# Deformable attention on one core: the stored dot products get two copies of their first and last line, and are read back in fewer pieces

## The chip, the cores and the metric

The kernel runs on one core of a Trainium2 chip. A core has TensorE (PE in the profile, its weight loads PEld), VectorE (DVE), ScalarE (ACT), GpSimd (POOL) and SyncE (SP), each with an instruction queue of its own that it works off in order. Here SP, ACT and POOL issue DMAs; sixteen DMA engines carry them out. The metric is the time on the device of one execution, in microseconds (us), as the median of several runs. Less is better.

## What is computed

The reference is two layers on x of shape (2, 64, 64, 256): a deformable attention, a graph-routed mixture of four experts, a shifted-window attention, and a mixture of eight experts. The change concerns the first of these. Cut to what matters, with eight groups g of 32 channels and nine sampling points k:

```
qkv = dwconv3x3(layernorm(x) @ qkv_w + qkv_b)
off[g]  = offsets from q, plus the 3x3 grid times (2g+1)
mask    = nine factors a pixel, from q
k_s     = bilinear(k_map[g], y + off_y, x + off_x) * mask     # 9 samples a pixel
v_s     = bilinear(v_map[g], y + off_y, x + off_x) * mask     # coordinates clipped to the image
attn    = softmax(q . k_s / sqrt(32))
out[g]  = sum over k of attn * v_s
x       = x + out @ proj_w + proj_b
```

Coordinates are clipped to the image: a sample above the first line takes the first line, one below the last takes the last.

## The kernel before, in words

The kernel samples without a gather. The offsets move a sample by less than one pixel from its grid place (the kernel has another path for the other case), so a sample is a weighted sum of 3x3 neighbours of that place. With r = 2g+1, a group needs key and value lines at y + (ky-1)r + sy-1 with ky and sy from 0 to 2: nine lines a row.

`static_attention` (line 470 on) runs n from -2 to 7 over the groups in the order 1, 2, ..., 7, 0. In each n it mixes three lanes of steps: the values of one group (`group_values`), the weights of the next (`group_weights`) and the dot products of the one after (`group_dots`). Each lane has a place in the order between 0 and 1 for each step (lines 515 to 525: values 0.12 + 0.88f, weights 0.04 + 0.8f, dots 0.95f), the steps are sorted by it and recorded. A scheduler that estimates durations then sets the final order on each engine and gives the DMAs of SP and ACT their completion semaphores.

`group_dots` (L538): `keys` and `queries` load key columns (L565) and query columns (L556) by SP. `multiply` (L570) forms, for two x at a time, the dot products of each of 64 rows (times 2 images: 128 partitions) with all 64 key lines and three neighbouring x on PE (L578), and copies them from PSUM to the tile `stage` on ACT (L585; in the first two n every second copy is DVE's). Eight such steps fill a tile of 64 lines x 3 x 32; two of these tiles are in use in turn. `store` (L590) writes them to the DRAM tile `dots` of the group from ACT's queue (L594): four DMAs of 16 rows, each with only those lines that its rows can need. A group has six such stores, group 0 four.

`group_weights` (L614): `read(ky)` (L672) picks, for each row y, its own three lines from `dots` into the tile `lk` (two in use), with all six column blocks. The address moves by one row and one line from one partition to the next, so rows of the same distance are one DMA of SP (`pick`, L655; L669). Where a line would lie outside the image the pick takes the first or last line; there the three lines are picked one by one, and the rows are cut where clipping begins and into multiples of 16 and a rest. `read_near` (L681) does it for group 0, five lines one by one. DVE multiplies the picked lines with bilinear weights and adds them up (L707, L711, L716, L720, L721), a softmax follows (L725 to L736), and DVE and POOL form the weights of the value lines (L746 to L776), which POOL writes to the DRAM tile `wd` (L786).

`group_values` (L854): SP loads values (L871), DVE spreads them (L876), POOL loads the weights of 16 rows in dense form (L882) into one of two `mat` tiles, and PE multiplies (L907) and accumulates over 18 columns and three kx. `clear` (L887) begins an accumulation with matmuls of a zero stationary operand `none` and, as moving operand, the first 512 columns of the constants `cstt`. ACT copies the sums out and stores them (L916, L919).

`cstt` holds constants of later stages; it is loaded at L206 at the very start and lies in SBUF to the end. `metaformer` (L2558) calls the stages: position table, first attention, projection and router, first experts, second attention, last experts.

Of the kernel before, what the change touches and what calls it, by code (L numbers as in the profile page):

```python
# [23 lines left out]
F32 = mybir.dt.float32  # L24
# [43 lines left out]
WB = W + 2 * BORDER  # L68
XH, XQ = W // 2, W // 4
ORDER = list(range(1, G)) + [0]  # L70
BAND = 16
# [122 lines left out]
class Net:  # L194
    def __init__(self, ctx, tc, I, out):
        self.tc, self.nc, self.I, self.out = tc, tc.nc, I, out
        self.const = ctx.enter_context(tc.tile_pool(name="const", bufs=1))
        nc = self.nc
        self.ident = self.const.tile([P, P], F32, name="ident")
        make_identity(nc, self.ident)  # L200
        self.colt = self.const.tile([P, NCOLS], F32, name="colt")
        nc.sync.dma_start(self.colt, I["cols"])
        self.rowt = self.const.tile([P, NROWS], F32, name="rowt")
        nc.scalar.dma_start(self.rowt, I["rows"].to_broadcast([P, NROWS]))
        self.cstt = self.const.tile([P, NCST], F32, name="cstt")
        nc.sync.dma_start(self.cstt, I["cst"])  # L206

# [330 lines left out]
    def group_dots(self, g, qd, kd, own, dots, pools, alone):  # L538
# [8 lines left out]
        runs = [(-2, 0), (1, 1)] if near else [((kx - 1) * r - 1, kx) for kx in range(3)]  # L547
        dots[g] = s = pools["dram"].tile([H, B, 6, H, 3, XH], F32, name="dots")
        two, steps, box = pools["first"], [], {}
# [20 lines left out]
        def multiply(h, dx, i0):  # L570
            kt, qt = box[h, dx], box["q", h]
            if i0 == 0:
                box["d"] = two.tile([P, H, 3, XH], F32, name="stage")
            ps = [pools["dot"].tile([P, 2, 3 * H], F32, name="dot") for _ in range(2)]
# [7 lines left out]
            for jj in range(2):  # L582
                x = XQ * jj + i0

                (nc.vector.tensor_copy if alone and jj else nc.scalar.copy)(  # L585
                    box["d"][:, :, :, x : x + 2],
                    ps[jj].rearrange("p i (s y) -> p y s i", s=3),
                )

        def store(h, at):  # L590
            for y in range(0, H, BAND):

                lo, hi = max(0, y - r - 1), min(H, y + BAND + r + 1)
                ins = nc.scalar.dma_start(  # L594
# [10 lines left out]
        for n, (h, dx, at) in enumerate(todo):  # L605
            if n == 1:
                steps.append(lambda: queries(1))
            if n + 2 < len(todo):
                steps.append(lambda n=n: keys(*todo[n + 2][:2]))
            steps += [lambda h=h, dx=dx, i=i: multiply(h, dx, i) for i in range(0, XQ, 2)]  # L610
            steps.append(lambda h=h, at=at: store(h, at))
        return steps

    def group_weights(self, g, offd, mask, low, edge, s, wd, none, pools):  # L614
# [39 lines left out]

        def pick(to, dy, first, blocks, n, y0=0, y1=H):  # L655

            for b in range(B):
                y = y0
                while y < y1:
                    ky = min(max(y + dy, 0), H - 1)  # L660
                    inside = 0 < y + dy < H - 1
                    end = min(y1, H - 1 - dy) if inside else (min(y1, 1 - dy) if y + dy <= 0 else y1)
                    if end - y > 16:
                        end -= (end - y) % 16
                    src = bass.AP(
                        s.tensor, s.offset + y * stride + b * (stride // B) + first * block + ky * line,
                        [[stride + (line if inside else 0), end - y], [block, blocks], [1, n * XH]],
                    )
                    nc.sync.dma_start(to[H * b + y : H * b + end], src)  # L669
                    y = end  # L670

        def read(ky):  # L672
            box[ky] = lk = two.tile([P, 6, 3, 3, XH], F32, name="lk")
            dy = (ky - 1) * r
            y0, y1 = max(0, 1 - dy), min(H, H - 1 - dy)
            pick(lk.rearrange("p k y s x -> p k (y s x)"), dy - 1, 0, 6, 9, y0, y1)
            for sy in range(3):
                for lo, hi in ((0, y0), (y1, H)):
                    pick(lk[:, :, sy].rearrange("p k s x -> p k (s x)"), dy + sy - 1, 0, 6, 3, lo, hi)

        def read_near():  # L681
# [172 lines left out]
    def group_values(self, g, vd, wd, mats, none, odd, sums, od, pools):  # L854
# [1703 lines left out]
def metaformer(ctx: ExitStack, tc: tile.TileContext, I, out):  # L2558
# [110 lines left out]
```

## Time and profile before

| | us |
|---|---|
| median of 3 runs | 5531.37 (5528.46 to 5539.13) |
| the profiled execution | 5531.03 |
| its span from first to last instruction | 5529.2 |

| stage, us from the start | length | PE | DVE | ACT | POOL | clock | DMA share | GB/s |
|---|---|---|---|---|---|---|---|---|
| 0 to 1090: edge sort, maps of q, k, v, offsets | 1090 | 937 | 822 | 178 | 96 | 0.88 | 0.61 | 131 |
| 1090 to 2470: first attention | 1380 | 960 | 400 | 314 | 478 | 0.81 | 0.74 | 187 |
| 2470 to 2660: projection, router | 190 | 96 | 74 | 19 | 37 | 0.74 | 0.52 | 143 |
| 2660 to 3500: graph edges | 840 | 404 | 339 | 24 | 399 | 0.72 | 0.16 | 30 |
| 3500 to 3780: first experts alone | 280 | 258 | 59 | 67 | 4 | 0.96 | 0.70 | 215 |
| 3780 to 5040: second attention beside experts | 1260 | 1136 | 635 | 568 | 247 | 0.94 | 0.44 | 135 |
| 5040 to 5529: last experts | 489 | 368 | 151 | 94 | 134 | 0.89 | 0.79 | 254 |

The columns of engines are busy us in the stage, clock is the share of full TensorE clock that was granted, and DMA share is the mean busy share of the sixteen DMA engines. An idle time of an engine is put down to what ended it: "PE dot L578 <- ACT stage L585: 209.5, 29, 27.9" reads as 209.5 us in 29 waits, the longest 27.9 us. A name with q (SPq, ACTq) is an engine's queue while it waits or issues a DMA, which does not count as busy.

### The profile page before, as it was taken

What the parts mean: (1) busy time and instruction counts of PE and PEld (TensorE: products, weight loads), DVE (VectorE), ACT (ScalarE), POOL (GpSimd) and SP (SyncE); (2) the same over time, 40 slices, a digit from 0 to 9 for tenths busy, and PEclk for the clock granted to TensorE, in tenths of its full rate; (3) what the DMA queues carried; (4) which work ended last, traced back from release to release, by engine and by line L of the source; (5) the groups of instructions that cost most, each with busy time, mean ns of one, the idle gap of its engine ahead of it and who ended that gap; (6) DMA issues with size and microseconds to landing.
All of it is one profiled execution on the core that took longest, in us unless ns stands there. A gap on an engine that the chain in (4) does not pass through costs nothing. (4 is left out here: it accounts for less than half of the span.)

```text
span 5529.2 us, 64325 instructions
## 1 busy us (share of the span) xinstructions
PE 4158.5 (75%) x22555; PEld 2930.8 (53%) x22555; DVE 2481.4 (45%) x5535; ACT 1264.3 (23%) x2432; POOL 1395.6 (25%) x1769
## 2 busy tenths in 40 slices
PE   7899999468677776554436670698999879998695
PEld 4565579355455554334213340586666546667584
DVE  5788888454322322203424481123444465543233
ACT  2221111022232222000200000123445344443121
POOL 3100000103344433422365406202120232101224
PEclk8898999668888888777768895899999889999898
DMA  8533368957888887665200003675454335445996
GB/s 227 169 118 105 104 138 82 118 152 182 208 210 216 210 225 178 151 144 164 13 5 5 4 1 108 207 232 185 130 148 120 94 119 155 131 127 155 306 308 202
DMA packets 752557, 808.72 MB, mean 146 GB/s; under 512 B 360516, under 2 KB 629280, under 8 KB 736466
## 3 DMA queue, kind: packets, MB, share of 16 engines
q1 hardware_dynamic: 590942, 477.93, 32.9%
q0 software_dynamic: 67552, 199.30, 14.5%
q10 hardware_dynamic: 93716, 127.14, 7.6%
q8 instruction: 184, 3.01, 0.2%
q14 instruction: 163, 1.34, 0.1%
HBM read 495.83 MB, written 312.33 MB: 146 GB/s over the span
## 5 line engine op out<-in xcount | busy, mean ns | idle before, releaser
L578 PE MATMUL dot<-kt,qt 64*128 64x192 f32 x2944 | 415.3, 398 | 322.0 <-ACT stage L585 209.5
L907 PE MATMUL acc<-mat,vt 128*64 128x192 f32 (+2 forms) x3680 | 531.8, 440 | 99.8 <-DMA mat<-wd 58.0
L578 PEld LDWEIGHTS dot<-kt,qt 64*128 64x128 f32 x2944 | 348.6, 227 | 418.6 <-ACT stage L585 243.8
L1415 PE MATMUL ps<-oh,ol 128*128 128x512 f32 (+1 forms) x864 | 358.0, 578 | 244.8 <-DVE oh L1408 166.8
L907 PEld LDWEIGHTS acc<-mat,vt 128*64 128x64 f32 x3680 | 300.6, 155 | 292.2 <-issue 185.7
L585 ACT COPY stage<-dot 128x384 f32<-128x384 f32 x640 | 275.7, 500 | 781.0 <-PE dot L578 446.9
L1415 PEld LDWEIGHTS ps<-oh,ol 128*128 128x128 f32 x864 | 179.0, 210 | 423.5 <-issue 307.0
L1689 PE MATMUL ps_h<-xgT,w1t 128*128 128x256 f32 x1216 | 320.1, 388 | 36.0 <-ACT hT L1692 25.4
L1825 PE MATMUL ps_y<-w2t,hT 128*128 128x256 f32 x1216 | 309.7, 406 | 41.7 <-ACT hT L1817 41.7
L1813 PE MATMUL ps_h<-xgT,w1t 128*128 128x256 f32 x1216 | 311.4, 399 | 34.9 <-ACT hT L1817 14.1
L1697 PE MATMUL ps_y<-w2t,hT 128*128 128x256 f32 x1216 | 305.8, 385 | 10.0 <-issue 8.8
L2432 POOL DMA_INDIRECT xs<-tn,sloti x128 | 124.3, 971 | 747.1 <-DVE slot L2430 676.4
L273 DVE SCALAR_TENSOR_TENSOR cv<-pad,colt,cv 128x2048 f32<-128x2048 f32 x128 | 298.8, 2348 | 0.0
L1825 PEld LDWEIGHTS ps_y<-w2t,hT 128*128 128x128 f32 x1216 | 239.0, 202 | 92.2 <-ACT hT L1817 48.4
L1813 PEld LDWEIGHTS ps_h<-xgT,w1t 128*128 128x128 f32 x1216 | 227.3, 196 | 99.8 <-ACT hT L1817 29.7
L1854 POOL DMA_INDIRECT back<-ys,back_row x128 | 134.3, 1049 | 560.6 <-DVE ex L1612 277.9
L437 PE MATMUL ps_k<-padk,diag 128*128 128x512 f32 x576 | 268.9, 626 | 0.2 <-ACT km L442 0.2
L1692 ACT ACTIVATE hT<-ps_h,b1t 128x256 f32<-128x256 f32 x304 | 143.9, 476 | 540.8 <-PE ps_h L1689 349.6
L1689 PEld LDWEIGHTS ps_h<-xgT,w1t 128*128 128x128 f32 x1216 | 230.0, 195 | 69.0 <-ACT hT L1692 27.5
L1697 PEld LDWEIGHTS ps_y<-w2t,hT 128*128 128x128 f32 x1216 | 234.5, 193 | 44.7 <-issue 10.3
L1299 PEld LDWEIGHTS <-ol 128*128 128x128 bf16 x1792 | 225.2, 148 | 38.7 <-issue 28.3
L1299 PE MATMUL psc<-oh,ol 128*128 128x64 bf16 x1792 | 236.4, 305 | 8.5 <-DVE oh L1297 8.5
(413 smaller groups left out, 6797.3 us busy)
## 6 DMA issues: line engine op xcount, KB each, us to landing
w1t<-in_W SPq DMA_DIRECT2D x152, 512.0 KB
w2t<-in_W SPq DMA_DIRECT2D x152, 512.0 KB
xg<-xs SPq DMA_DIRECT2D x152, 256.0 KB
kt<-kd SPq DMA_DIRECT2D x92, 288.0 KB
pr<-stage SPq DMA_DIRECT2D x16, 1584.0 KB
mat<-wd POOLq DMA_DIRECT2D x56, 384.0 KB
b2t<-in_b SPq DMA_DIRECT2D x152, 128.0 KB
ys<-y ACTq DMA_DIRECT2D x76, 256.0 KB
```

The lines of the kernel that those rows point to most:

```text
L273: nc.vector.scalar_tensor_tensor(out, src, w, out, ALU.mult, ALU.add)
L437: nc.tensor.matmul(ps.rearrange("p a b -> p (a b)"), lhsT=diag[:, tap, :], rhs=pad[:, at : at + 8, tap % 3 : tap % 3 + W], start=(tap == 0 ...
L578: nc.tensor.matmul(ps[jj][:, i, :], lhsT=qt[at, i0 + i].rearrange("p y b -> p (y b)"), rhs=kt[at, i0 + i : i0 + i + 3, :].rearrange("p s y ...
L585: (nc.vector.tensor_copy if alone and jj else nc.scalar.copy)(box["d"][:, :, :, x : x + 2], ps[jj].rearrange("p i (s y) -> p y s i", s=3),)
L907: nc.tensor.matmul(sums[h][64 * q : 64 * q + 64, j - 2 + a : j - 2 + c, :].rearrange("p x y -> p (x y)"), lhsT=vt[:, r + 1 + XH * h + XQ * ...
L1299: nc.tensor.matmul(psc, lhsT=ol[:, :, j], rhs=oh[:, :, j], start=(c1 == 0), stop=(c1 == NW - 1),)
L1415: nc.tensor.matmul(psf[:, c : c + m], lhsT=ol, rhs=ohf[:, c : c + m], start=(start and j == 0), stop=(stop and j == n - 1),)
L1689: nc.tensor.matmul(ps, lhsT=w1t[:, k, f * P : (f + 1) * P], rhs=xT[:, k, :], start=(k == 0), stop=(k == CC - 1),)
L1692: nc.scalar.activation(hT[:, f, :], ps, AF.Gelu, bias=b1t[:, f : f + 1])
L1697: nc.tensor.matmul(ps, lhsT=hT[:, f, i * P : (i + 1) * P], rhs=w2t[:, f, :], start=(f == 0), stop=(f == NF - 1),)
L1813: nc.tensor.matmul(ps[:, f % 2], lhsT=box["w1"][:, k, f * P : (f + 1) * P], rhs=box["xT"][:, k, :], start=(k == 0), stop=(k == CC - 1),)
L1825: nc.tensor.matmul(ps[:, i], lhsT=box["hT"][:, f, i * P : (i + 1) * P], rhs=box["w2"][:, f, :], start=(f == 0), stop=(f == NF - 1),)
```

## The change

A stored row block of `dots` now has 68 lines instead of 64: two copies of the first line, the 64 lines, two copies of the last. `multiply` fills the middle, a new step `sides` makes the copies with two ACT instructions before each store, and `store` writes the copies with those bands of rows that reach an end. With them the three lines around a clipped place always lie behind each other, so `read` needs at most four pieces an image: rows before the image's first line (all with the same address of line), a multiple of 16 rows inside, the rest, and rows past the last line. `read_near` takes all five lines of 64 rows in one DMA, for two images, two halves of the width and two parts of columns. So that the larger tiles fit, `cstt` is no longer held during the first attention: it is allotted and loaded after it, and `clear` uses `none`, repeated four times, as the moving operand. Line numbers after the edits move by a few.

```diff
+SIDE = 2
+HS = H + 2 * SIDE
...
-        self.cstt = self.const.tile([P, NCST], F32, name="cstt")
-        nc.sync.dma_start(self.cstt, I["cst"])
...
-        dots[g] = s = pools["dram"].tile([H, B, 6, H, 3, XH], F32, name="dots")
+        dots[g] = s = pools["dram"].tile([H, B, 6, HS, 3, XH], F32, name="dots")
...
-                box["d"] = two.tile([P, H, 3, XH], F32, name="stage")
+                box["d"] = two.tile([P, HS, 3, XH], F32, name="stage")
...
-                    box["d"][:, :, :, x : x + 2],
+                    box["d"][:, SIDE : SIDE + H, :, x : x + 2],
...
+        def sides():
+            d = box["d"].rearrange("p k s x -> p k (s x)")
+            for to, at in ((0, SIDE), (SIDE + H, SIDE + H - 1)):
+                nc.scalar.copy(d[:, to : to + SIDE], d[:, at : at + 1].to_broadcast([P, SIDE, 3 * XH]))
+
...
-                lo, hi = max(0, y - r - 1), min(H, y + BAND + r + 1)
+                lo, hi = max(0, y - r - 1 + SIDE), min(HS, y + BAND + r + 1 + SIDE)
+                lo, hi = (0 if lo <= SIDE else lo), (HS if hi >= SIDE + H else hi)
...
+            steps.append(sides)
             steps.append(lambda h=h, at=at: store(h, at))
...
-        def pick(to, dy, first, blocks, n, y0=0, y1=H):
-
-            for b in range(B):
-                y = y0
-                while y < y1:
-                    ky = min(max(y + dy, 0), H - 1)
-                    inside = 0 < y + dy < H - 1
-                    end = min(y1, H - 1 - dy) if inside else (min(y1, 1 - dy) if y + dy <= 0 else y1)
-                    if end - y > 16:
-                        end -= (end - y) % 16
...
-                    nc.sync.dma_start(to[H * b + y : H * b + end], src)
-                    y = end
+        srow, sblock = B * 6 * HS * 3 * XH, HS * 3 * XH
 
         def read(ky):
             box[ky] = lk = two.tile([P, 6, 3, 3, XH], F32, name="lk")
+            to = lk.rearrange("p k y s x -> p k (y s x)")
             dy = (ky - 1) * r
-            y0, y1 = max(0, 1 - dy), min(H, H - 1 - dy)
-            pick(lk.rearrange("p k y s x -> p k (y s x)"), dy - 1, 0, 6, 9, y0, y1)
-            for sy in range(3):
-                for lo, hi in ((0, y0), (y1, H)):
-                    pick(lk[:, :, sy].rearrange("p k s x -> p k (s x)"), dy + sy - 1, 0, 6, 3, lo, hi)
+            y0, y1 = max(0, -dy), min(H, H - dy)
+            whole = y0 + (y1 - y0) // 16 * 16
+            parts = ((0, y0, 0, 0), (y0, whole, y0 + dy + SIDE - 1, line), (whole, y1, whole + dy + SIDE - 1, line), (y1, H, H - 1 + SIDE, 0))
+            for b in range(B):
+                for lo, hi, at, more in parts:
+                    if lo < hi:
+                        src = bass.AP(
+                            s.tensor, s.offset + lo * srow + b * (srow // B) + at * line,
+                            [[srow + more, hi - lo], [sblock, 6], [1, 9 * XH]],
+                        )
+                        nc.sync.dma_start(to[H * b + lo : H * b + hi], src)
...
-            for y in range(5):
-                pick(lk[:, y, :, 0:3].rearrange("p h s x -> p h (s x)"), y - 2, 0, 2, 3)
-                pick(lk[:, y, :, 3:5].rearrange("p h s x -> p h (s x)"), y - 2, 2, 2, 2)
+            for b in range(B):
+                for h in range(2):
+                    for first, at, n in ((0, 0, 3), (2, 3, 2)):
+                        src = bass.AP(
+                            s.tensor, s.offset + b * (srow // B) + (first + h) * sblock,
+                            [[srow + line, H], [line, 5], [1, n * XH]],
+                        )
+                        nc.sync.dma_start(lk[H * b : H * b + H, :, h, at : at + n].rearrange("p y s x -> p y (s x)"), src)
...
-                    sums[h][:, x : x + 8, :].rearrange("p x y -> p (x y)"), lhsT=none, rhs=self.cstt[:, 0:512],
+                    sums[h][:, x : x + 8, :].rearrange("p x y -> p (x y)"), lhsT=none, rhs=none.unsqueeze(1).to_broadcast([P, 4, P]),
...
+    net.cstt = rp.tile([P, NCST], F32, name="cstt")
+    tc.nc.sync.dma_start(net.cstt, I["cst"])
```

More of the change, by code (lines that the diff above doesn't have):

```diff
@@ L653, in group_weights @@
         stride, block, line = B * 6 * H * 3 * XH, H * 3 * XH, 3 * XH
-        def pick(to, dy, first, blocks, n, y0=0, y1=H):
-            for b in range(B):
-                y = y0
-                while y < y1:
-                    ky = min(max(y + dy, 0), H - 1)
-                    inside = 0 < y + dy < H - 1
-                    end = min(y1, H - 1 - dy) if inside else (min(y1, 1 - dy) if y + dy <= 0 else y1)
-                    if end - y > 16:
-                        end -= (end - y) % 16
[L665 to L669, printed above, removed]
-                    y = end
+        srow, sblock = B * 6 * HS * 3 * XH, HS * 3 * XH
         def read(ky):
             box[ky] = lk = two.tile([P, 6, 3, 3, XH], F32, name="lk")
+            to = lk.rearrange("p k y s x -> p k (y s x)")
             dy = (ky - 1) * r
-            y0, y1 = max(0, 1 - dy), min(H, H - 1 - dy)
-            pick(lk.rearrange("p k y s x -> p k (y s x)"), dy - 1, 0, 6, 9, y0, y1)
-            for sy in range(3):
-                for lo, hi in ((0, y0), (y1, H)):
-                    pick(lk[:, :, sy].rearrange("p k s x -> p k (s x)"), dy + sy - 1, 0, 6, 3, lo, hi)
+            y0, y1 = max(0, -dy), min(H, H - dy)
[9 more added lines that the diff above has]
+                        nc.sync.dma_start(to[H * b + lo : H * b + hi], src)
         def read_near():
```

## The prediction, made before the changed kernel was run

> **What bounds the kernel now.** I took the busy time by stage first, then the waits of the first attention, then ACT's order of time in one place, and SP's list of DMAs there. The edit sits in the stage from 1090 to 2470 us; its steady part is 1300 to 2250 us. Columns of the stretches: span, then busy us of PE, its weight loads, DVE, ACT and POOL with counts, granted TensorE clock, DMA share, GB/s.
>
> ```profile
> 1450.00:1500.00 50.00, 16.09 (x122) 14.94 (x124) 16.93 (x22) 15.05 (x34) 7.10 (x14) 0.64 0.84 204
> 1600.00:1650.00 50.00, 26.13 (x188) 20.92 (x186) 8.78 (x13) 14.43 (x33) 1.96 (x4) 0.73 0.75 207
> 1850.00:1900.00 50.00, 50.00 (x369) 30.38 (x366) 11.40 (x12) 16.98 (x39) 31.28 (x55) 1.00 0.94 262
> 1300.00:2250.00 950.00, 719.34 (x5130) 477.34 (x5129) 257.28 (x319) 257.86 (x577) 346.11 (x591) 0.86 0.80 204
> ```
>
> Once in about 165 us (1450, 1610, 1780, 1950, 2120) no engine is full: that is where one group of heads follows the other. Between these PE is full. PE's own waits in 1400 to 2230 us and those of SP's queue:
>
> ```profile
> PE dot L578 <- ACT stage L585: 196.2, 19, 27.9
> ...
> SPq L669 <- DMA lk<-dots: 76.0, 40, 11.3
> SPq L669 <- DMA dots<-stage: 71.2, 6, 60.2
> ```
>
> So PE waits for ACT's evictions. ACT in order of time at one such change of groups (start, us, what, count, idle before):
>
> ```profile
> 1597.62 5.53 ACTq L594 DMA_DIRECT2D dots<-stage  x4
> ...
> 1611.58 3.98 ACTq L919 DMA_DIRECT2D od<-o  x2
> 1615.60 1.64 ACT L585 COPY stage<-dot 128x384 f32<-128x384 f32 x4 [10.62 <-DMA qt<-qd]
> ...
> 1629.95 7.04 ACTq L594 DMA_DIRECT2D dots<-stage  x4
> 1637.03 1.64 ACT L585 COPY stage<-dot 128x384 f32<-128x384 f32 x4 [14.55 <-DMA lk<-dots]
> ...
> 1660.98 4.54 ACTq L594 DMA_DIRECT2D dots<-stage  x4
> 1665.62 1.65 ACT L585 COPY stage<-dot 128x384 f32<-128x384 f32 x4 [19.98 <-DMA dots<-stage]
> ```
>
> ACT ends its copies at 1622.5 and 1645.6, yet can issue the stores of L594 only at 1629.95 and 1660.98. In the built program all DMAs of SP and ACT take eight completion semaphores in turn, and each waits until the previous one on its semaphore has landed. The trace shows which that was: a pick of 48 rows that SP issued at 1625.40, then one of 9 rows from 1652.36. Adding up these waits over 1300 to 2250 us by the semaphore's last user, I find ACT's stores 194 us behind picks (32 waits). SP's picks of groups 1 to 7 (ns shortest, median, longest; first and last start), over all and in this one place:
>
> ```profile
> L669 SPq DMA_DIRECT2D lk<-dots x306: 233/633/4012, 1192.4 to 2160.5; - x153
> ...
> L669 SPq DMA_DIRECT2D lk<-dots x44: 265/492/707, 1605.4 to 1660.5; - x44
> ```
>
> Forty-four picks take SP from 1605.4 to 1660.5, and ACT's store queue is tied to their pace. That is the stall.
>
> **The change, part by part.** The sum is made against the profiled run, 5531.03 us (span 5529.2); the median of the runs is 5531.37, so they are one number.
>
> *Fewer picks.* In the built order of the changed kernel the picks of groups 1 to 7 fall from 306 to 98 (14 a group: 6, 2, 6), those of group 0 from 64 to 8. The place above, worked again: the first picks still wait for the landing of the last stores (1610.1, 1613.3), od still waits for the query loads (1615.6). Eight picks at 0.6 us leave SP by 1619; I take 5 us for landing, 1624. ACT, done at 1622.5, issues its store at about 1624 instead of 1629.95 and copies its next chunk by about 1635 instead of 1645.6. The third read waits for the buffer of the first: DVE works that off in 6 x 0.757 + 2 x 0.357 = 5.3 us, so six picks leave at 1630 to 1633 and land at 1638; the second store goes at 1638 instead of 1660.98, and copies resume at about 1641 instead of 1665.62. That is 25 us. The bytes do not shrink, though: at 207 GB/s now and 262 where DMA is fullest, the 68 us from 1597.6 to 1665.6 cannot go below 68 x 207/262 = 54, a gain of 14. I take 16, as neighbouring stretches can lend DMA time. Five places: -80, between 0 (another load holds the semaphores) and -125.
>
> [...]
>
> *First group.* Its picks run 31 us (1192.4 to 1223) with little else in SP's queue, and its weights start PE's value matmuls at 1299.7. With 14 picks DVE's last third starts about 12 us earlier: -10 (0 to -12).
>
> *The tail, group 0.* After 2252 nothing is left beside it:
>
> ```profile
> 2301.58 21.14 PE L907 MATMUL acc<-mat,vt 128*64 128x64 f32 x160 [36.69 <-DVE vt L876]
> ...
> 2419.03 21.16 PE L907 MATMUL acc<-mat,vt 128*64 128x64 f32 x160 [25.12 <-DMA mat<-wd]
> ```
>
> The value map for 2301.58 was loaded at 2294.7, behind the 64 picks in SP's queue; the weights for 2419 follow DVE's last third at 2297.9, also behind picks. The last stores, ready at 2229.8, waited 13.2 us for a pick. With eight picks they go at 2230, land by 2240, the picks by 2250; the offsets are worked on from 2256 (biases and reduction take until 2263, as now), and three uninterrupted passes of DVE of 5.3 us end at 2279 instead of 2307. POOL's 90 us behind that stay. That is 28; I take -25 (0 to -35).
>
> *Two copies of a line, each store.* 46 stores, 92 new ACT copies of 128x192. The nearest rows: 500 ns for 128x384 (issued every 0.375) and 1.15 us for an ACT pass of 128x1152 from SBUF; so 0.25 us each, 0.5 a store, 23 us on ACT, which is 23% busy here. It counts where ACT's copies are the path: three stores in each of five changes of groups and the twelve of the start: 27 x 0.5 = +13 (5 to 23). Behind it in ACT's queue stand the store itself and the next evictions, for which PE waits.
>
> *Bigger stores.* Lines stored rise from 67.7 to 70.3 MB; 2.6 MB at 207 GB/s is 12 us of DMA time, spread over 1100 us: +4 (0 to 12).
>
> *Constants.* One load of 258 KB leaves SP's start and goes ahead of the projection's loads at 2473; at 200 GB/s 1.3 us, and DVE's first users have until 2526: +1 (-1 to 5). Zeros as both operands of the 64 clearing matmuls: same shape, same count, 0.
>
> *Order elsewhere.* The late stage (3780 to 5040 us) is put in another order, with 15 more table loads on ACT at 1.283 us, 19 us in all; ACT is 45% busy and PE 90% there: +5 (0 to 19). The start (0 to 1090 us) keeps its work in a slightly different order: 0 (-15 to 15).
>
> Sum: -80 - 10 - 25 + 13 + 4 + 1 + 5 = -92; 5531 - 92 = 5439, say 5440.
>
> **The rivals.**
> 1. DMA bandwidth takes most of it. For: the loop already moves 204 GB/s at a share of 0.80. Against: 0.75 in the stalls. The stretches then gain 6 us each, the tail 15: -30 - 5 - 15 + 23 = -27, 5504.
> 2. Slower: the lane stays shut. In the changed order 53 of the 184 store DMAs still follow a pick on their semaphore, 55 before, and those picks are now mostly large ones. If their landing and not their number set the 194 us, nothing is gained, and ACT pays 13 for copies, 4 for bytes, and up to 19 for table loads: +36, 5567. It decides when the wait before a store at a change of groups stays above some 30 us in sum (194/5 = 39 now). Against: SP issued the pick of 48 rows at 1472.57, late behind others, when ACT had already waited.
> 3. The copies hide a full gain: -125 - 12 - 35 + 15 = -157, 5374.
>
> **How the numbers follow.** As forecast (5410 to 5480) 0.62; rival 1 (5480 to 5520) 0.18; no difference 0.04; rival 2 0.11; rival 3 (below 5410) 0.05. Within 0.2% (11 us) is about what a measurement here can't tell from no change: same 0.04, faster 0.85, slower 0.11. From 5390 to 5512 lie about 8 in 10.
>
> **What would show it.** Right: about 106 picks; PE's wait for ACT at the changes of groups from 196 to below 110 us; ACT's stores behind picks below 80 us; DMA above 215 GB/s in the loop; PE's 36.69 us gap gone. Wrong: the low stretches keep their length with another load named as releaser, or the late stage grows by over 15 us.

## The result, and the profile after

The changed kernel takes 5489.15 us in the median of four runs (5487.4 to 5501.39), the kernel before, run beside it, 5530.02: a ratio of 0.993 (95% interval 0.9917 to 0.9942), 41 us less. The forecast was 5440. The profiled execution took 5501.39 us, span 5499.6; it is the longest of the four.

Stretches of the changed kernel, columns as before. The first two lie in the change of groups that the prediction worked through (now at 1609 to 1663 us), the third between two changes, the last is the steady part:

```profile
1600.00:1650.00 50.00, 27.41 (x184) 22.78 (x184) 12.82 (x13) 19.65 (x44) 12.00 (x21) 0.73 0.92 239
1630.00:1670.00 40.00, 14.33 (x102) 12.64 (x104) 20.98 (x32) 10.25 (x25) 0.00 (x0) 0.66 0.90 230
1850.00:1900.00 50.00, 50.00 (x335) 29.46 (x334) 8.52 (x8) 18.45 (x43) 28.57 (x47) 1.00 0.92 269
1300.00:2250.00 950.00, 744.69 (x5176) 494.28 (x5178) 275.05 (x354) 281.85 (x651) 359.82 (x613) 0.86 0.83 217
```

PE is still half idle at the change, but the DMA engines are not: share 0.75 before, 0.90 to 0.92 now. The steady part moves 217 GB/s, above the 215 that the prediction named as a sign. PE's waits in 1400 to 2230 us, then those of SP's queue:

```profile
PE dot L578 <- ACT stage L585: 141.2, 18, 28.8
```

```profile
SPq L691 <- DMA dots<-stage: 73.6, 2, 73.2
...
SPq L678 <- DMA lk<-dots: 37.1, 7, 11.9
...
SPq L678 <- DMA qt<-qd: 26.2, 10, 7.2
```

PE's wait for ACT's evictions fell from 196.2 to 141.2 us, not below 110; SP's picks wait half as long for older picks (76.0 to 37.1). ACT in order of time at that change of groups:

```profile
1608.75 0.35 ACTq L600 DMA_DIRECT2D dots<-stage  x1
...
1627.21 1.40 ACT L585 COPY stage<-dot 128x384 f32<-128x384 f32 x3 [0.40 <-PE dot L578]
1628.64 0.60 ACT L593 COPY stage<-stage 128x192 f32<-128x192 f32 x2
1638.60 4.85 ACTq L600 DMA_DIRECT2D dots<-stage  x4
1643.57 1.64 ACT L585 COPY stage<-dot 128x384 f32<-128x384 f32 x4 [14.32 <-DMA lk<-dots]
...
1651.52 0.60 ACT L593 COPY stage<-stage 128x192 f32<-128x192 f32 x2
1658.84 4.51 ACTq L600 DMA_DIRECT2D dots<-stage  x4
1663.47 1.66 ACT L585 COPY stage<-dot 128x384 f32<-128x384 f32 x4 [11.34 <-DMA lk<-dots]
```

L593 are the two new copies. Take the place as the prediction's floor does, from the issue of the store ahead of it (1597.62 before, 1608.75 now) to the evictions behind its second store (1665.62 and 1663.47). It took 68.0 us and takes 54.7, which is 13 us less. The prediction found 25 us from the stores, a floor of 54 us from the bytes (14 less), and took 16. The same two stretches, before and changed:

```profile
1597.60:1665.60 68.00, 35.56 (x254) 26.04 (x250) 18.29 (x26) 14.43 (x33) 4.00 (x9) 0.76 0.79 203
```

```profile
1608.70:1663.40 54.70, 26.03 (x184) 21.56 (x180) 14.76 (x21) 16.25 (x40) 3.93 (x8) 0.72 0.96 246
```

Inside the place the course was not the forecast one. Count from the end of the evictions ahead of the first of the two stores (1622.5 before, 1628.6 now). The first store went after 7.4 us before, was forecast after 1.5, and goes after 10.0. The second went after 38.5, was forecast after 15.5, and goes after 30.2. Evictions resumed after 43.1, were forecast after 18.5, and resume after 34.9. So 8 of the 13 us lie here; the other 5 lie ahead of these evictions. SP's picks (ns shortest, median, longest; first and last start), over all, and SP in order of time at this place:

```profile
L678 SPq DMA_DIRECT2D lk<-dots x98: 233/346/4094, 1200.0 to 2129.3; - x98
```

```profile
1616.33 14.27 SPq L678 DMA_DIRECT2D lk<-dots  x7
...
1633.87 0.59 SPq L678 DMA_DIRECT2D lk<-dots  x1
...
1654.46 2.15 SPq L678 DMA_DIRECT2D lk<-dots  x6
```

There are 98, as counted beforehand, and at the change above they take SP from 1616.3 to 1656.6 us, 40 us in place of 55. The first eight alone take 18 us, where 5 were forecast: the picks now wait for completion semaphores of query loads (`qt`, 7.2 us at the longest). ACT's stores behind picks, added up as in the prediction, fell from 194 to 101 us. Of the waits over 0.5 us behind the picks of groups 1 to 7 there are 24 as before, of 4.1 us each in place of 7.3: the waits did not go away, they got shorter. In the tail PE's long gaps are:

```profile
2248.18 10.68 PE L911 MATMUL acc<-mat,vt 128*64 128x64 f32 x80 [35.80 <-DMA mat<-wd]
...
2295.97 10.69 PE L911 MATMUL acc<-mat,vt 128*64 128x64 f32 x80 [25.95 <-DMA mat<-wd]
...
2371.32 21.13 PE L911 MATMUL acc<-mat,vt 128*64 128x64 f32 x160 [23.18 <-DMA mat<-wd]
```

The gap of 36.69 us is not gone: one of 35.80 stands there, put down to the weights of the values (`mat`) instead of to the value map.

A second pair of profiles exists from chips on which the later stages are faster: the changed kernel again, and the kernel before with only the constants moved, which costs nothing (below). Stage by stage, in us:

| | before, changed | constants only, changed again |
|---|---|---|
| start to first dot product | 1107.2, 1112.8 | 1107.0, 1106.1 |
| first group | 192.5, 194.3 | 192.6, 187.2 |
| loop, first addition to last dot product | 929.5, 891.6 | 931.1, 884.1 |
| tail | 234.9, 217.7 | 225.3, 216.7 |
| projection | 161.2, 161.0 | 162.1, 162.8 |
| behind it | 2903.9, 2922.2 | 2608.3, 2609.2 |
| sum of the differences | -29.6 | -60.3 |

The +5.6 at the start and +18 at the end are not seen in the second pair; the first profile came from a run 12 us above its fellows. What the change does lies in the attention: loop -38 and -47, tail -17 and -9, first group +2 and -5. The border between loop and tail is not quite the same everywhere: in the first profile of the kernel before, one block of 80 additions (10.7 us) more lies behind the last dot product than in the other three. With that block on the same side the first pair reads -49 in the loop and -6 in the tail, close to the second.

### The profile page after: what moved, and what is told of

It is laid out like the page before. It is cut to its first block, busy times and chain, and to the rows that moved or that the text cites. A ratio compares the mean times of both kernels' runs of the same rounds, so it can differ in the third digit from the quotient of the medians.

```text
span 5499.6 us, 64161 instructions
## 1 busy us (share of the span) xinstructions
PE 4197.9 (76%) x22555; PEld 2941.3 (53%) x22555; DVE 2480.4 (45%) x5535; ACT 1309.3 (24%) x2540; POOL 1391.4 (25%) x1769
## 5 line engine op out<-in xcount | busy, mean ns | idle before, releaser
L578 PE MATMUL dot<-kt,qt 64*128 64x192 f32 x2944 | 431.7, 400 | 245.8 <-ACT stage L585 153.9
L1701 PE MATMUL ps_y<-w2t,hT 128*128 128x256 f32 x1216 | 304.0, 383 | 18.0 <-issue 16.8
L1829 PE MATMUL ps_y<-w2t,hT 128*128 128x256 f32 x1216 | 297.6, 393 | 22.3 <-ACT hT L1821 17.2
L1829 PEld LDWEIGHTS ps_y<-w2t,hT 128*128 128x128 f32 x1216 | 229.0, 194 | 77.6 <-issue 20.5
L1701 PEld LDWEIGHTS ps_y<-w2t,hT 128*128 128x128 f32 x1216 | 233.1, 192 | 51.7 <-issue 17.6
L1303 PEld LDWEIGHTS <-ol 128*128 128x128 bf16 x1792 | 225.3, 148 | 47.4 <-issue 40.1
```

The costliest lines, as they stand in the source:

```text
L578: nc.tensor.matmul(ps[jj][:, i, :], lhsT=qt[at, i0 + i].rearrange("p y b -> p (y b)"), rhs=kt[at, i0 + i : i0 + i + 3, :].rearrange("p s y ...
L1303: nc.tensor.matmul(psc, lhsT=ol[:, :, j], rhs=oh[:, :, j], start=(c1 == 0), stop=(c1 == NW - 1),)
L1701: nc.tensor.matmul(ps, lhsT=hT[:, f, i * P : (i + 1) * P], rhs=w2t[:, f, :], start=(f == 0), stop=(f == NF - 1),)
L1829: nc.tensor.matmul(ps[:, i], lhsT=box["hT"][:, f, i * P : (i + 1) * P], rhs=box["w2"][:, f, :], start=(f == 0), stop=(f == NF - 1),)
```

## The experiments

Chips differ: on some the kernel before takes 5520 to 5537 us, on others 5218 to 5220, and that difference lies behind the projection. Ratios are therefore to the kernel before on the same chip, and lengths of the attention (first dot product to last addition) are compared across all. Two profiles of the changed kernel itself have 1303.6 and 1288.0 us there, so a difference of that size between two single profiles shows nothing. Below, "the changed kernel" means ratio 0.9908 (0.9890 to 0.9925) where the kernel before took 5218 to 5220, and 0.993 where it took more.

**The changed kernel again.** No edit.

> The changed kernel once more, for its profile and time on the chip on which the next three run. Ratio to before 0.993 as at first; attention from the first dot product to the last addition 1304 us (1357 before). If the profiled run at first was a poor one after the attention (12 us above its other runs), the stage from the second attention's end to the end of the kernel is again about 561 us, not 579.

Measured 5167.33 against 5218.35, 51 us less, ratio 0.9908. Attention 1288.0 us. From the last output product of the second attention to the end it is 508 us, not the 522 of the first profile.

**Constants alone.** The kernel before, with:

```diff
-        self.cstt = self.const.tile([P, NCST], F32, name="cstt")
-        nc.sync.dma_start(self.cstt, I["cst"])
...
-                    sums[h][:, x : x + 8, :].rearrange("p x y -> p (x y)"), lhsT=none, rhs=self.cstt[:, 0:512],
+                    sums[h][:, x : x + 8, :].rearrange("p x y -> p (x y)"), lhsT=none, rhs=none.unsqueeze(1).to_broadcast([P, 4, P]),
```

and the load behind the attention, as in the change.

> The kernel before with only the smallest part of the change: the table of constants is loaded behind the attention and the clearing multiplications move the zeros themselves. My reckoning for this part was +1 us, with 15 more table loads of the scalar engine late in the kernel (+5 for order elsewhere). If the part is without price: ratio to before 1.000 (within 0.002), first dot product at 1106-1108 us, everything behind the projection 2600-2612 us as in the other runs on these chips. If it costs what the first profile of the changed kernel showed (start +5.6, end +18): ratio 1.003 to 1.005.

Ratio 1.0000 (0.9988 to 1.0013). This part, and the other order of the late stage, are free.

**Each copy three times.**

```diff
-                nc.scalar.copy(d[:, to : to + SIDE], d[:, at : at + 1].to_broadcast([P, SIDE, 3 * XH]))
+                for _ in range(3):
+                    nc.scalar.copy(d[:, to : to + SIDE], d[:, at : at + 1].to_broadcast([P, SIDE, 3 * XH]))
```

> Each of the two copies of the first and last line is done three times: 184 more copies of the kind that took 0.35 us (64 us of scalar-engine time). If the copies lie on the path ahead of the stores in full, the attention part gets 64 us longer (5553); at half of the stores, as I reckoned for the prediction (0.25 us each on 27 x 0.5 stores of the loop, 46 in all), about 20-30 us; if they are hidden by other waits of the scalar engine, under 10.

Ratio 0.9945 (0.9927 to 0.9963), 19 to 23 us above the changed kernel. The 184 more copies (median 347 ns) add 64 us of busy ACT, of which a third reaches the end. By proportion, which is an estimate, the change's own 92 cost 10 to 11 us; forecast were 13.

**Two picks a read.**

```diff
-            parts = ((0, y0, 0, 0), (y0, whole, y0 + dy + SIDE - 1, line), (whole, y1, whole + dy + SIDE - 1, line), (y1, H, H - 1 + SIDE, 0))
+            parts = ((0, H, ky, line),)
```

> Each read is fetched by two picks of 64 rows (all of one diagonal, so that a row's lines are not those it needs: the logits, and what the router then sends to whom, differ) in place of four or six; the bytes and the lines per row are the same. 98 picks become 42 in seven groups. Theory A (what still delays a group change is the landing of the third read, which waits for the buffer of the first, and the stores that take the completion semaphores just behind its picks): only two of eight semaphores are then taken by picks, so the scalar engine's waits behind picks fall from about 100 to under 50 us in the loop, and the loop from 892 to 865-880 us, but the third read's picks still issue as late as now (about 25 us after the second read's). Rival N (number of picks alone, some 0.19 us for each that was removed: 41 us by 208): 56 fewer give 10 us in all, loop 880. Rival B (the transfers' bandwidth, 0.84 of the span now): same bytes, so the loop stays at 888-895 whatever the waits do.

Ratio 0.9859 (0.9836 to 0.9882): 20 to 26 us below the changed kernel, more than number at 0.19 us each would give. Stores behind picks waited 53 us in 14 waits, nearly as theory A had it (under 50). The loop is 872.4 us, in theory A's range, but here too one block of 80 additions (10.7 us) lies in the tail instead; the attention as a whole is 1272.1 us. PE's wait for evictions stayed at 138 us in 1400 to 2200 (141 in the changed kernel), so that the shorter waits behind picks are not the whole of it.

**Pieces of 16 and of 32 rows.** Ahead of the loop over images in `read`, with 16 or 32:

```diff
+            parts = [(a, min(a + 16, hi), at + (a - lo if more else 0), more) for lo, hi, at, more in parts for a in range(lo, hi, 16)]
```

> The long picks are cut in pieces of 16 rows: the same lines by 196 picks in place of 98 in seven groups, bytes the same. Rival N (number): half of the picks that the change took away come back, so some 18-20 us of the 41 come back: about 5508, loop 910. Theory A (landing of the third read, not number): at most the sequencer's 14 x 0.6 us = 8 us for each group change if it lies on the path, else little: loop 892-905. Rival B (bandwidth): no change in bytes, 0-5 us.

> The long picks are cut in pieces of 32 rows: eight picks a read in all three reads (4 + 4 edge pieces in the outer ones), 140 in seven groups in place of 98, bytes the same; with pieces of 16 rows it was 8 and 10 a read, 196 in all, and the whole gain was gone. Theory W (waves: DMAs that the sync engine may have in flight are bounded by eight completion semaphores, so a read of more than eight picks must see its first ones land before its last go): eight picks still go in one wave, so at most 10 us of the 41 come back: 5489-5500 or a ratio to before of 0.993-0.995. Rival N (number alone, 0.42 us a pick as between 98 and 196): 42 more picks give back 18 us, ratio 0.9965.

With 16 rows (10 + 8 + 10 picks a group): ratio 1.0007 (0.9998 to 1.0016); the whole gain is gone, with 196 picks in place of the 306 of before. PE's wait for evictions in 1400 to 2200 us is back:

```profile
PE dot L578 <- ACT stage L585: 185.4, 21, 29.3
```

But the stores' waits behind picks are not back: they add up to 107 us, where the changed kernel has 97 (second profile) and the kernel before 194. So the wait that the prediction was built on explains only a part of this loss. With ACT's record laid beside PE's waits, PE waits 44 us more than in the changed kernel; in 16 of them ACT waits behind a pick, in 15 it is issuing stores, in 10 it waits behind `raw`.

With 32 rows (8 + 4 + 8; the expectation says eight in all three, but the middle read has four): 0.9917 (0.9902 to 0.9932), 5 to 10 us worse. That looked like a threshold at eight picks a read, theory W, so I tried it with one or two reads cut.

**Only the outer reads in pieces of 16, and only the middle one.** The line above under `if ky != 1` (10 + 2 + 10) and under `if ky == 1` (6 + 8 + 6).

> Only the first and third read are cut in pieces of 16 rows: 10 + 2 + 10 picks a group, 154 in seven groups. Theory W (waves: a read of more than eight picks waits for its own first ones to land): nearly the whole loss of the run with 10 + 8 + 10 (56 us against the changed kernel on chips of like speed) must come back here, 30 us or more: ratio to before 0.996-1.000. Rival N (number alone, 0.57 us a pick by that run): 56 picks give 32 us as well, but then the next run loses 24; by the run with 8 + 4 + 8 (10 us for 42 picks, 0.23 us each) 13 us: ratio 0.993.

> Only the middle read is cut in pieces of 16 rows: 6 + 8 + 6 picks a group, 140 in seven groups, as many as in the run with 8 + 4 + 8. Theory W: no read has more than eight, so at most 10 us come back: ratio 0.991-0.993. Rival N at 0.57 us a pick: 24 us, ratio 0.9955.

Ratios 0.9966 (0.9955 to 0.9977) and 0.9960 (0.9945 to 0.9975): 20 and 17 us above the changed kernel, the same within their intervals, although one has reads of more than eight and the other not. The threshold of theory W falls.

**Number alone.** Behind each read's picks:

```diff
+            for i in range(4 * ky, 4 * ky + 4):
+                nc.sync.dma_start(pools["spare"][:, i], s[i : i + 1, 0, 0, 2, 0, 0:4])
```

> The changed kernel with four more DMAs of 16 bytes behind each read's picks, into a buffer that nobody reads: 84 more DMAs in seven groups on the sync engine's queue and on the shared semaphores, no bytes to speak of. If the number of DMAs on these queues is what counts (0.2 to 0.5 us each, as 42 to 98 more picks cost 5 to 52 us): 20-40 us slower than the changed kernel, ratio to before 0.997-1.000 on a chip of the first kind (0.993 there), 0.995-0.998 on one of the other (0.991). If it was the form of the picks (16 rows each) that cost: under 10 us.

Ratio 0.9935 (0.9914 to 0.9956), the changed kernel's. 84 more DMAs on SP's queue and on the shared semaphores cost nothing that can be measured. One reservation: their data is there earlier than the picks', and the scheduler set 36 of them ahead of the changes of the loop (1134 to 1362 us). The other 48 stand in changes, most of them behind the picks of a third read, as here:

```profile
1646.95 2.14 SPq L679 DMA_DIRECT2D lk<-dots  x6
1649.13 5.57 SPq L681 DMA_DIRECT2D spare<-dots  x8
```

ACT's stores waited 11 us behind them in all. So the plain number is close to free; this does not show that as many DMAs among the picks of the first two reads would be.

**Picks from GpSimd's queue.**

```diff
-                        nc.sync.dma_start(to[H * b + lo : H * b + hi], src)
+                        nc.gpsimd.dma_start(to[H * b + lo : H * b + hi], src)
```

> The 98 picks of the seven groups are issued by GpSimd in place of the sync engine; same DMAs, same bytes. GpSimd's DMAs use other completion semaphores than those that the sync and scalar engines share. Theory W (semaphores shared by picks and stores): the scalar engine's waits behind picks, 95 us in the loop, go to none, the idle time of the matrix engine before dot products falls from 141 to under 80 us; but the loads of mat and the weights stand behind the picks' wait for the stores on GpSimd, so additions may wait more. Net -10 to -30 us if the cover is good (ratio 0.985-0.989); if GpSimd's order costs more than that, over 0.992. Rival (the sequencer's time for issuing is what counts, on whichever engine): dot products wait as much as now.

Ratio 0.9912 (0.9898 to 0.9927), no gain, but the waits have moved just as theory W's first half has it. PE's and POOL's waits, 1300 to 2200 us:

```profile
PE acc L911 <- DMA mat<-wd: 76.4, 8, 25.7
POOL lk L678 <- DVE lg L725: 68.3, 4, 29.8
...
PE dot L578 <- ACT stage L585: 60.8, 17, 7.6
POOL mat L886 <- DMA lk<-dots: 51.8, 24, 5.6
```

No store waits behind a pick any more; PE's wait before dot products falls to 60.8 (141.3 in the changed kernel). In exchange the loads of `mat`, now behind the picks on POOL's queue and its semaphores, wait 51.8 us for picks, POOL 68.3 for the buffer, and PE 76.4 for `mat` (9.7 in the changed kernel). This shows the tie through queue and semaphores directly. It also shows that PE's wait before dot products is not the price: 80 us less of it, and the kernel is no faster.

**A third buffer, and the third read early; then late.** The third read takes the tag of the weights, of the same size:

```diff
-            box[ky] = lk = two.tile([P, 6, 3, 3, XH], F32, name="lk")
+            box[ky] = lk = two.tile([P, 6, 3, 3, XH], F32, name="lk", tag="wt" if ky == 2 else "lk")
```

In the early form `read(2)` also stands right behind `read(1)` in the steps.

> The third read of a group gets a buffer of its own (the tag that the weights use later in the group, same size), and its picks are placed with the second read's ones, so that they wait for no multiply of the first read. Nothing of the result changes. Theory A: the third read's picks issue within 10 us of the second read's, and the 14.5, 11.6, 13.2, 28.4 and 28.8 us gaps of the matrix engine near the group changes shrink by half: loop 892 to 845-870 us, time 5440-5470. Rival B (bandwidth): the reads come earlier but the queues are as full; the loop stays within 10 us, 5480-5495. A loss is possible where 28 picks in one row hold all eight semaphores longer: then the scalar engine's waits behind picks grow over 100 us and the loop over 900.

> The third read has a buffer of its own as in the run with the third buffer, but its place in the order of steps stays where the changed kernel has it (after the first read's additions), so that its picks are not set ahead of the second read's multiplications. If the loss of that run (27 us against the changed kernel on chips of like speed) came from 14 picks standing in one row ahead of the stores: no loss here, and up to 15 us gain where the vector engine's release of the first read's buffer was the wait (ratio to before 0.988-0.992). If the loss came from the buffer that it shares with the weights: again ratio 0.994-0.996.

Early: ratio 0.9945 (0.9926 to 0.9965), 19 to 27 us worse. The third read's multiplication did start earlier (35 us behind the group's first pick, 43 in the changed kernel, means of seven groups), and the loop still grew to 926.5: PE's wait for evictions went to 158.3 us in 1400 to 2200 (141.3), the stores' waits on semaphores from 122 to 162 us. The growth is not behind the picks (97 and 100 us) but behind loads of key columns (`kt`, 24 and 53 us); why these hold the stores longer is not shown. Late: 0.9926 (0.9914 to 0.9938), 9 to 13 us worse, no gain. The wait for the first read's buffer is real (15.3 us of SP's queue behind DVE's L725 in the changed kernel, four waits in 1400 to 2230 us), but theory A, that it holds the change, falls.

**Half of each `mat` load.**

```diff
                 lo, hi = band(g, y)
+                hi = lo + (hi - lo) // 8 * 4
```

> Each load of the gathered matrices (mat) brings only half of its lines; the other lines keep what the buffer held, so the sums, and what the router then sends to whom, differ. Some 35 of the loop's 197 MB are not moved. Rival B (bandwidth takes what the picks gave): the loop shortens by 60 us or more beyond the changed kernel (892 to under 830), the group changes as well as the stretches between. Theory W (semaphores and landing): the group changes hold their length to within a third (146 us of idle matrix engine), and the loop falls by under 40 us, mostly in the tail where loads of mat are waited for (36, 26 and 23 us gaps there).

Ratio 0.9777 (0.9761 to 0.9793), 64 us below the changed kernel. The DMA share of 1300 to 2200 us falls to 0.73, and PE's wait for evictions (second fence, 1400 to 2200 us) with it, though no pick and no store was touched:

```profile
1300.00:2200.00 900.00, 745.89 (x5233) 487.24 (x5231) 276.42 (x364) 281.73 (x651) 354.39 (x613) 0.90 0.73 195
```

```profile
PE dot L578 <- ACT stage L585: 115.7, 21, 15.6
```

The stores' waits behind picks over 0.5 us go from 95 to 75 us. Loop 851.9 (-32) and tail 193.2 (-24): less than rival B said, and within what theory W had (under 40 in the loop, PE's wait at the changes to within a third). The bytes that move beside the picks are a part of the stall; that it is by the landing time of a pick fits, but was not measured by itself.

**The value map by GpSimd; with it, the copies by the vector engine; with it, the third buffer (late).**

```diff
-                    nc.vector.tensor_scalar(vt[:, x : x + n, b, :], raw[:, 0:n, :], odd[:, b : b + 1], None, ALU.mult)
+                    nc.gpsimd.tensor_scalar(vt[:, x : x + n, b, :], raw[:, 0:n, :], odd[:, b : b + 1], None, ALU.mult)
```

> The multiplications that write the value map (vt) go to GpSimd in place of the vector engine, so that their wait for the transfer of raw (14-21 us) stands no longer ahead of the first read's steps, nor ahead of the last third of the weights in the tail. Theory A (what is left at a change hangs on the vector engine's order): loop 10-30 us shorter than 892, tail 8-14 us shorter than 218. Rivals W and B: within 8 us in all; or a loss of up to 20 us where the loads of mat, which GpSimd issues, then stand behind the wait for raw.

> The changed kernel with two edits together: the value map is written by GpSimd (alone: ratio to before 0.988 against the changed kernel's 0.991), and the copies of the first and last line are made by the vector engine, which that frees. The run with each copy three times was 23 us slower by chips of like speed than the changed kernel, for 184 copies: 0.12 us each, so the 92 copies of the change cost 11 us of the path. If they are hidden on the vector engine: ratio 0.985-0.987, about 5142. If a store then waits for a busy vector engine: 0.988-0.992.

> The value map written by GpSimd (alone 12 us faster than the changed kernel) together with the third read's own buffer at the old place in the order (alone 5-10 us slower by ratio, though its first group was 6 us shorter). If the vector engine's order was what spoiled the second, the two give 15-25 us together: ratio 0.986-0.988 on a chip like the one of the value-map run; if not, 0.989-0.992.

Ratios 0.9878 (0.9860 to 0.9896), 0.9904 (0.9890 to 0.9918) and 0.9985 (0.9970 to 1.0000; this one where the changed kernel has 0.993). The first is the fastest version that leaves nothing out, 12 us below the changed kernel, though their intervals touch; of these only 5 lie in the attention (1283.0 to 1288.0), the rest behind it, where nothing but order differs. Its loop is 808 us and its tail 291, since 400 additions more lie behind the last dot product: the waits moved. The parts do not add up. A new order by the scheduler with each edit may be the cause; no run shows it apart.

**Fewer picks with uneven rows.** The middle of the outer reads in one piece of 61 to 49 rows (4 + 2 + 4 picks a group), alone and with the value map by GpSimd:

```diff
-            whole = y0 + (y1 - y0) // 16 * 16
+            whole = y1
```

> The middle of the outer reads is no longer cut at a multiple of 16 rows: 4 + 2 + 4 picks a group, 70 in seven groups, same bytes and same result. The run with two picks a read (42 in all) was 20 us faster than the changed kernel; 28 of those 56 picks go here. By number 10 us (ratio 0.989); by theory W, fewer semaphores held by picks, 5-15 us (0.988-0.990). If transfers of 49 to 61 rows are slower than 48 and a rest (their rows don't divide over the DMA engines evenly): no gain or a loss to 0.995.

> The run before (4 + 2 + 4 picks) with the value map written by GpSimd too, which alone gave 12 us: if the two add up, 0.986 or below (5145); if they take the same wait, 0.988.

Ratios 1.0342 (1.0321 to 1.0362) and 1.0393 (1.0376 to 1.0410): the first some 228 us slower than the changed kernel, with 28 DMAs fewer. What happened is in the section on the hardware.

## Why the prediction was half right

*The direction was right, and the mechanism in part.* Fewer picks shortened the stores' waits, and with them PE's. The run with the picks on GpSimd shows the tie; the run with pieces of 16 rows shows that the gain hangs on the cut of the picks, since 196 of them give all of it back. That run also shows that the stores' wait behind picks is not all of the price, since there it hardly grew.

*The step that failed is the size of two terms: the five changes of groups, -80, and the tail, -25.* With the loop's copies and larger stores the loop stood at about -70 net; measured are -38 and -47. The issue times of the stores let the five changes be measured as at the place above, and the stretches between them too (us in all, from the twelfth store to the forty-fourth):

| | before | constants only | changed | changed again | half of `mat` | 16 rows | picks on GpSimd |
|---|---|---|---|---|---|---|---|
| five changes | 359 | 347 | 296 | 295 | 259 | 314 | 237 |
| between them | 436 | 458 | 463 | 457 | 449 | 489 | 496 |

The changes gave -63 and -51, copies included, where -72 had been put (-80, and 7.5 for fifteen stores' copies). The stretches between, put at nothing but a part of the +4 for bytes, went by +27 and -2. The kernel before and the one with constants only, of equal time, differ by 12 and 22 in these rows, so the division is rough. The working said that eight picks would leave SP by 1619, land by 1624, and let the store go. The picks left slowly and landed late. One change of the changed kernel shows it whole, SP, DVE and ACT in order of time, 1913 to 1977 us:

```profile
1925.08 9.78 SPq L678 DMA_DIRECT2D lk<-dots  x8
1934.96 0.56 SPq L875 DMA_DIRECT2D raw<-vd  x1
...
1961.06 6.34 SPq L678 DMA_DIRECT2D lk<-dots  x6
```

```profile
1947.71 2.10 DVE L711 TENSOR_TENSOR lk<-lk,tents 128x576 f32<-128x576 f32 x3 [6.60 <-DMA lk<-dots]
...
1956.41 1.42 DVE L880 TENSOR_SCALAR vt<-raw,edge 128x1024 f32<-128x1024 f32 x2 [5.93 <-DMA raw<-vd]
```

```profile
1948.34 0.60 ACT L593 COPY stage<-stage 128x192 f32<-128x192 f32 x2
1971.89 5.06 ACTq L600 DMA_DIRECT2D dots<-stage  x4
1977.12 1.65 ACT L585 COPY stage<-dot 128x384 f32<-128x384 f32 x4 [28.18 <-DMA dots<-stage]
```

The second read's two picks of 64 rows, issued at 1933.5, are not multiplied before 1947.7; `raw`, issued at 1935, is there at 1956.4; both stand in DVE's queue ahead of the rest of the first read, so that the buffer for the third read comes free at 1961, not 5.3 us after the first landing. ACT's store, ready at 1948.9, takes semaphores just behind the third read's picks and goes at 1971.9. I had costed a landing at 5 us, for which the prediction names no run; here it is 11 to 21 from issue to use, at a DMA share of 0.90 over 1950 to 2000 us. Giving the third read its own buffer did not help; taking bytes away did, and at the changes (295 to 259 us in the table).

*The floor from bandwidth was the better forecast.* I let the changes reach the 262 GB/s of the fullest stretch, 14 us, and took 16 on the ground that neighbouring stretches can lend DMA time. The place worked through came to 54.7 us against the floor of 54, at 246 GB/s and a share of 0.96. The same sum for all five, an estimate with each change's own rate before (194 to 215 GB/s) against 262, gives 277 us; measured are 296, at 228 to 264 GB/s and shares of 0.90 to 1.01 (the share as the profile counts it can pass 1). Between changes the fullest stretch has 269 GB/s at 0.92, so at a change the DMA engines move fewer bytes in the same busy time. With what was lost between the changes, a fifth of the loop's -38 to -47, a change gave 8 to 9 us. Rival 1, with 6 us each and 5504, was nearer to the first measurement. What a DMA more costs was not one number: 84 small ones gave the changed kernel's own ratio (0.9935), but 98 more cuts of the same bytes cost 51 to 56 us.

*Rival 2, the lane stays shut,* named the right obstacle: 24 stores wait behind a pick as before. It was wrong that landing alone sets the sum; each wait shrank from 7.3 to 4.1 us.

*First group:* -10, with 6 of its twelve stores' copies against it, so -4; measured +2 and -5. *Tail:* -25; measured -17 and -9, or -6 and -9 for the same work, as PE's gaps there now end with `mat`. *Copies:* +13, by the tripled copies 10 to 11. *Bigger stores:* not measured by themselves. *Constants, late stage, start:* +6, measured 0.

*What stays open.* How the price grows with the cut of the picks: 42 more cost 5 to 10 or 17 us, 56 cost 20, 98 cost 51 to 56, and the 306 of before no more than the 196; neither a price for each nor a threshold at eight fits. Whether the difference between 42 in one form and in the other is more than the scheduler's order was not told apart. Nor is it known why most of what the pieces of 16 rows cost lies between the changes (32 of 51 us in the table).

## What to carry to other kernels

Ask of each queue not only how many DMAs it issues but which completion semaphore each one takes, and who stands behind it: a store can wait for another engine's load with which it shares no data. Here SP's and ACT's DMAs shared eight semaphores (2404 DMAs in the trace before, 2140 after) and POOL's had eight others (184 each), and ACT's stores waited 194 us behind SP's picks before and 101 after. When such a stall is to be priced, take the landing time from the trace of that very stretch (5 us were costed, 11 to 21 passed from issue to use at a DMA share of 0.90), and expect the freed bytes to collide: a stretch with PE half idle at a DMA share of 0.79 could be shortened by a fifth, and then stood at 0.96. An engine's wait that goes away is not time saved until the stretches beside it are measured too: with the picks on GpSimd PE waited 80 us less before its dot products, at a ratio of 0.9912 against 0.9908. And fewer transfers of the same bytes can cost more: 98 picks, the long ones of 48 rows in the outer reads, gave a ratio of 0.993, and 70 with 49 to 61 rows in one piece 1.0342.

## What the runs showed of the hardware

In the kernel with the uncut middle the DMA engines are busy for a share of 0.20 to 0.32 while DVE and ACT wait. Stretches in three groups with 61, 59 and 53 rows, then DVE's and ACT's waits from 1190 to 2360 us:

```profile
1250.00:1290.00 40.00, 7.42 (x32) 5.89 (x31) 2.53 (x7) 2.88 (x7) 0.00 (x0) 0.54 0.20 53
1450.00:1500.00 50.00, 19.40 (x129) 12.52 (x125) 3.47 (x8) 6.04 (x14) 1.93 (x4) 0.70 0.29 79
1985.00:2020.00 35.00, 6.16 (x36) 5.87 (x36) 0.00 (x0) 3.86 (x9) 0.00 (x0) 0.55 0.32 78
```

```profile
DVE lk L711 <- DMA lk<-dots: 339.5, 11, 52.0
ACT stage L585 <- DMA lk<-dots: 180.2, 6, 53.7
```

From the first issue of the third read to its first multiplication it takes, by the rows of its long pick:

| rows | 61 | 59 | 57 | 55 | 53 | 51 | 49 |
|---|---|---|---|---|---|---|---|
| uncut, us | 42.1 | 47.4 | 24.2 | 13.8 | 40.5 | 20.1 | 13.6 |
| uncut, value map by GpSimd, us | 42.8 | 47.1 | 15.5 | 8.5 | 56.2 | 25.6 | 24.6 |
| cut at 48, us | 11.4 | 7.9 | 8.7 | 9.1 | 10.8 | 17.9 | 8.1 |
| packets of picks in flight, uncut | 1 | 1 | 3 | 11 | 1 | 3 | 7 |

The slow ones are the primes 61, 59 and 53, in both kernels: 40.5 to 56.2 us, where the other lengths took 8.5 to 25.6. The last row is the number of packets of picks (1152 bytes each) that the trace of the first has most often in flight at one moment of the third read, when there are any. With 1 in flight the first kernel took 40.5 to 47.4 us, with 3 it took 20.1 and 24.2, with 7 and 11 it took 13.6 and 13.8, and each of these numbers divides the rows of its pick. The traces do not name the engine of a packet, so how the rows were shared among the engines was not shown.
